# Four layers of graph network on 16 graphs: where the sort, the first graph's gates and the stores stand beside the attention

## The chip, the cores and the metric

The kernel runs on one core of one Trainium2 chip. The metric is the device time of one execution in microseconds (us). Before the change: 14,099.2 us, the median of three runs (14,098.43 to 14,108.07).

The engines, as the profile names them: PE is TensorE's matmuls and PEld its weight loads; DVE is VectorE; ACT is ScalarE; POOL is GpSimd; SP is SyncE, which here only issues DMA transfers. SPq, ACTq and POOLq are the queues from which the engines issue them.

## The reference

Sixteen graphs of 1024 nodes with 64 features each; `adj` is 16 x 1024 x 1024 float32. Each layer's result is added to its input and layer-normed.

```python
x = _layernorm(x + _L0_gnn_ref(x, adj, ...))            # normalised propagation, leaky ReLU
x = _layernorm(x + _L1_gnn_ref(x, adj, ...))            # attention
x = _layernorm(x + _L2_gnn_ref(x, adj, nodemask, ...))  # quantiles of the neighbours' features, MLP
x = _layernorm(x + _L3_gnn_ref(x, adj, ...))            # propagation
```

Layer 1 has 8 heads of 64. Its scores are gated by each node's own `gamma`, and the adjacency by the other half of it:

```python
gamma = jnp.exp(x @ W_gamma.T + b_gamma)
attn = g0 * attn + g1 * adj[:, None]
attn = jax.nn.softmax(attn, axis=-1)
out = jnp.einsum('bhnm,bhmd->bnhd', attn, v).reshape(b, n, H * DIM)
return out @ W_proj.T + b_proj
```

Layer 2 thins out each node's neighbours, sorts every feature over the remaining ones (`jnp.sort(vals, axis=2)`), and mixes the quantiles 0.25, 0.5 and 0.75 into an MLP with 128 hidden units.

## The kernel before

The graphs go through in eight pairs, and the outer loop over `p` runs stages of three pairs at once. Iteration `p` builds, in this order of the program: layer 0 of pair `p`, graph 0 and then graph 1 (`layer0`, with the thinning of the neighbours in `neighbours`); behind each of these graphs, layers 2 and 3 of one graph of pair `p - 2` (`ends`, `layers23`); the attention of pair `p`; the sort of pair `p - 1` (`middle`, `sort`); and pair `p - 1`'s quantile stage (`quantiles`). Iterations 0 and 1 have no `ends`, iteration 0 no sort and no quantiles, iteration 8 no layer 0 and no attention.

A planner puts this into order when the program is built: every instruction has its place in the program as its priority, and each engine gets a fixed list, drawn from the planner's own estimate of when inputs and buffers will be there. On the chip each engine works through its list and waits where an input isn't there. A manual dependency without a semaphore (`add_manual_dep` with `in_order`) holds one instruction behind another of the same engine in that list. Tiles come from pools with a number of buffers each; `bank` is a pool of four PSUM tiles that nearly every stage uses, `banks` one of two larger ones. Pools in SBUF share addresses over time: a tile waits for the tiles that lay where it lies.

**Attention.** For each graph of the pair, `keys_of` transposes x1, `gates` computes `gm` (L448 products, L452, the exponential L453) and the gated copy `xg` (L457), `queries_of` transposes that (both transposes are L277, their copies L278), and `gated` multiplies a block of the adjacency by its gate on GpSimd (L465). Then 64 steps follow: graph, head pair `hp` (4), half of the nodes `nh` (2), block `k4` (4). A step's parts on TensorE are put in sequence by hand (`then`): the scores of a step to come (L495, two heads), the transposes of this step's exponentials (L514), here and there a projection (L474) or values (L486), and at `k4 == 3` the scores of one step more and 32 products with the values (L522). Scores go through VectorE (L502: add the adjacency, row maximum) and ScalarE (L504: exponential), the transposes back through ScalarE (L516). `heads` (L537 to L547) multiplies by the output weights, sums over heads, and for `k == 3` adds bias and x1 and norms the layer into x2. At the end x2 is stored (L598), transposed (L603), copied (L604) and stored again as x2T (L605), both stores on SyncE's queue. The first graph's gates stand ahead of step 0, the second's at steps 10, 12 and 15.

**Sort.** A bitonic network over 1024 values in 55 steps, all on VectorE (L1034): three instructions a step (compare, minimum, maximum), each mask stored to DRAM, then the same 55 steps backwards on ranks with four instructions a step, each mask loaded again: 385 "swaps". `pace` holds every L502 of the attention, two per step:

```python
n = 4 * (next(steps_v) - EARLY) // 13
if 0 <= n < len(pace):
    tc.add_manual_dep(i.ins, pace[n].ins.name, in_order, reason="pace of the sort")
```

So the first `EARLY = 60` swaps are free and then 13 follow each two steps. Behind the sort the ranks are transposed (L1079, a `bank`), copied (L1081) and turned into words on VectorE (L1082 to L1102); `middle` is built behind the whole attention.

**Quantiles.** `load_matrix` loads the thinned adjacency `ndT` (8 loads on SyncE's queue); `elements` makes the one-hot words E from the words (L735 to L740, seven buffers); the first six half words are matmuls L808; then 96 steps of compare (L814), one-hot (L823), pick (L831) and matmuls L799, with the values' sums (L861, L880).

Of the kernel before, what the change touches and what calls it, by code (L numbers as in the profile page):

```python
# [25 lines left out]
P = 128  # L26
# [21 lines left out]
SECOND = (26, 28, 30, 38, 40, 45, 46, 47)  # L48
AHEAD = (10, 12, 15)
STEPS = 55  # L50
EARLY = 60
BN_EPS = 1e-5
# [57 lines left out]
def gnn_kernel(ctx: ExitStack, tc: tile.TileContext, a: dict, out: bass.AP):  # L110
# [147 lines left out]

    def layernorm(dst, y):

        st = small.tile([P, 4, 2, 6], F32, name="ln_st")
        mv = small.tile([P, 4, 2, 2], F32, name="ln_mv")
        rs = small.tile([P, 4, 2], F32, name="ln_rs")
        blocks = [(k, f) for k in range(4) for f in range(2)]
        for k, f in blocks:
            nc.vector.bn_stats(st[:, k, f, :], y[:, k, f, :])
            nc.vector.bn_aggr(mv[:, k, f, :], st[:, k, f, :])
        nc.scalar.activation(rs, mv[:, :, :, 1], AF.Sqrt, bias=eps)
        nc.vector.reciprocal(rs, rs)
        for k, f in blocks:  # L270
            nc.vector.tensor_scalar(dst[:, k, f, :], y[:, k, f, :], mv[:, k, f, 0:1], rs[:, k, f:f + 1],
                                    op0=ALU.subtract, op1=ALU.mult)
# [152 lines left out]
    def attention(nat, ip, adj, x1, x2):  # L425
# [4 lines left out]
        with (tc.tile_pool(name="att", bufs=2, reuse_waits="tile") as att,  # L430
              tc.tile_pool(name="att1", bufs=1, reuse_waits="tile") as att1):
            wqkv = twice(att1, "wqkv", a["WqkvT"], 3 * H * C)
# [3 lines left out]

            class Graph(SimpleNamespace):
                pass

            def keys_of(gr):  # L440
                gr.xT = att.tile([P, 512], F32, name="xT")
                transposed(gr.xT, gr.x1, then)

            def gates(gr):
                ps = [bank([P, 4, 2]) for f in range(2)]
                for k in range(4):
                    for f in range(2):
                        then(nc.tensor.matmul(ps[f][:, k, :], gr.xT[HALF[f], k * P:(k + 1) * P], wg[HALF[f]],  # L448
                                              start=True, stop=True))
                gr.gm = small.tile([P, 4, 2, 2], F32, name="gm")  # L450
                for f in range(2):
                    nc.vector.tensor_tensor(gr.gm[:, :, f], ps[f], bg_r[:, None, :].to_broadcast([P, 4, 2]), ALU.add)  # L452
                nc.scalar.activation(gr.gm, gr.gm, AF.Exp)  # L453
                gr.xg = att.tile(NODES, F32, name="xg")
                for k in range(4):
                    for f in range(2):
                        nc.vector.tensor_scalar(gr.xg[:, k, f, :], gr.x1[:, k, f, :], gr.gm[:, k, f, 0:1], C ** -0.5,  # L457
                                                op0=ALU.mult, op1=ALU.mult)

            def queries_of(gr):  # L460
                gr.xgT = att.tile([P, 512], F32, name="xgT")
                transposed(gr.xgT, gr.xg, then)

            def gated(gr, k):
                nc.gpsimd.tensor_scalar(gr.adj[k], gr.adj[k], gr.gm[:, k % 4, k // 4, 1:2], 1.0,  # L465
                                        op0=ALU.mult, op1=ALU.mult)
# [24 lines left out]
            def scores(gr, hp, k):  # L491
# [7 lines left out]
                for h in range(2):  # L499
                    s = att.tile([P, N], F32, name="s", bufs=4)  # L500
                    mx = att.tile([P, 1], F32, name="mx", bufs=4)
                    pace.append(nc.vector.tensor_tensor_reduce(  # L502
                        s, ss[h], gr.adj[k], -1.0, 3.0e38, ALU.add, ALU.min, mx))
                    nc.scalar.activation(s, s, AF.Exp, bias=mx, scale=-1.0,  # L504
                                         accum_out=gr.sm[:, k, 2 * hp + h:2 * hp + h + 1])
                    exps.append(s)
                return exps
# [19 lines left out]
            def heads(gr, k):  # L527
# [15 lines left out]
                nc.vector.tensor_reduce(gr.xg[:, k], t.rearrange("p f h q c -> p f c (h q)"), AX.X, ALU.add)  # L543
                if k == 3:
                    nc.vector.tensor_tensor(gr.xg, gr.xg, over_nodes(bp_r), ALU.add)
                    nc.vector.tensor_tensor(gr.xg, gr.xg, gr.x1, ALU.add)
                    layernorm(by_half(x2)[:, :, :, gr.bb, :], gr.xg)  # L547

            graphs = [Graph(bb=bb, x1=x1[bb], adj=list(adj), qk={}, sm=att.tile([P, NB, H], F32, name="sm"))
                      for bb in range(2)]  # L550
            g0, g1 = graphs
            keys_of(g0)
            gates(g0)
            queries_of(g0)
            for k in range(NB):
                gated(g0, k)
# [11 lines left out]
            for st, (gr, hp, nh, k4) in enumerate(steps):  # L568
# [7 lines left out]
                if at < 4:  # L576
                    if gr is g1:
                        heads(g0, at)
                    values(gr, at)
                if st in AHEAD:  # L580
                    (keys_of, gates, queries_of)[AHEAD.index(st)](g1)
# [16 lines left out]
            nc.sync.dma_start(x2_d[ds(ip * P, P)], x2)  # L598
# [6 lines left out]
            nc.sync.dma_start(x2T_d[ds(ip * P, P)], x2T)  # L605
        return pace
# [136 lines left out]
    def quantiles(ip, rk, u_w, b_w):  # L743
# [12 lines left out]
        with ExitStack() as es:  # L756
# [155 lines left out]
            load_matrix(graphs[0])  # L912
            more_words(2 * NW, nc.tensor.matmul)
# [61 lines left out]
    def layers23(agg1, agg2, tof, ip, bb):  # L975
# [16 lines left out]
        hT = agg1.tile([P, N], F32, name="hT")  # L992
# [6 lines left out]
        y = agg1.tile(NODES, F32, name="y2")  # L999
# [9 lines left out]
        sup = agg1.tile(NODES, F32, name="sup")  # L1009
# [14 lines left out]

    def sort(pool, key, pace, rk, u_w, b_w):
# [5 lines left out]
        steps_v = count()  # L1031

        def swap(*args):
            i = v.tensor_tensor(*args)  # L1034
            n = 4 * (next(steps_v) - EARLY) // 13
            if 0 <= n < len(pace):
                tc.add_manual_dep(i.ins, pace[n].ins.name, in_order, reason="pace of the sort")
# [39 lines left out]
        ps = bank([P, NB, P], F16)  # L1077
        for k in range(NB):
            nc.tensor.transpose(ps[:, k, :], rank[:, k * P:(k + 1) * P], identh)  # L1079
        r16 = pool.tile([P, 2 * G, NB, 4], U16, name="r16")  # L1080
        nc.scalar.copy(r16.rearrange("p g j c -> p j g c"), ps.rearrange("p j (g c) -> p j g c", c=4))  # L1081
        v.tensor_scalar(rk, r16, 5, None, op0=ALU.logical_shift_right)  # L1082
        v.tensor_scalar(r16, r16, 31, None, op0=ALU.bitwise_and)

        m = pool.tile([P, 2 * G, NB, 4], U16, name="m16")
        e = pool.tile([P, 2 * G, NB, 4], U16, name="e16")
        z = pool.tile([P, 2 * G, NB, 4], U16, name="z16")
        for w, first in ((2, 18), (1, 4), (0, 0)):
            dst = z if w == 0 else b_w[w - 1].bitcast(U16)
            if w < 2:  # L1090
                v.tensor_scalar(m, r16, float((4, 18)[w]), None, op0=ALU.is_lt)
            if w == 2:
                v.tensor_scalar(e, r16, 18.0, None, op0=ALU.is_ge)
            elif w == 1:
# [52 lines left out]
    for p in range(B // 2 + 1):  # L1147
        with double_banks(), ExitStack() as es:
# [20 lines left out]
            if p >= 1:  # L1169
                middle(srt, key, pace)  # L1170
# [35 lines left out]
```

## Time and profile before

| | us |
|---|---|
| median of three runs | 14,099.2 |
| the profiled execution | 14,101.11 |
| its span on the core | 14,099.3 |
| TensorE matmuls busy | 12,501.2 (89%) |
| VectorE busy | 10,732.0 (76%) |
| ScalarE busy | 7,312.0 (52%) |
| GpSimd busy | 598.3 (4%) |
| granted TensorE clock, mean | 0.937 |
| sort, L1034, all pairs | key 572.5, rank 391.6, mask 304.0, d 208.5 + 187.1 |
| attention's L502 / L504 | 1,211.9 / 1,179.4 |

A window line of the profile gives a stretch in us from the span's start, its length, then for each engine busy us and the number of instructions (waiting ones of the engine's sequencer included in a window of one line), the granted clock as a share of full speed, the mean share of the DMA engines, and GB/s. A timeline line gives start, duration, engine, line, operation, result and inputs, shapes, the number of merged instructions, and in brackets how long the engine was idle before and what ended that. A wait line gives who waited for whom, the total in us, how often and the longest.

The stages of one middle pair, from the lines' first and last times: layer 0 with layers 2 and 3 from 4102 to 4315, attention from 4315 to 4835, quantiles from 4845 to 5836. The pairs' first L808 products start at 1370.5, 3111.4, 4845.2, 6572.3, 8313.1, 10,053.8, 11,791.1 and 13,008.2; the sort of iteration 8, with no attention beside it, runs from 12,747 to 12,997.

### The profile page before, as it was taken

How to read it: one execution, taken by the hardware profiler on the slowest of the kernel's cores; microseconds unless marked ns; L12 is line 12 of the kernel's file. 1: busy time of each engine (PE TensorE's matmuls, PEld its weight loads, DVE VectorE, ACT ScalarE, POOL GpSimd, SP SyncE). 2: the span in 40 equal slices, each digit the busy share in tenths (PEclk: the TensorE clock that was granted, in tenths of full speed). 3: DMA queues.
4: the chain of work that ended last, by engine and by line, in shares of the span. 5: the costliest groups of instructions: out<-in, count | busy, mean ns of one | idle time of the engine just before them, and what ended most of it. 6: DMA issues, size and time to landing. Idle time of an engine off the chain costs nothing.

```text
span 14099.3 us, 207608 instructions
## 1 busy us (share of the span) xinstructions
PE 12501.2 (89%) x81450; PEld 5279.4 (37%) x81536; DVE 10732.0 (76%) x18475; ACT 7312.0 (52%) x13288; POOL 598.3 (4%) x932
## 2 busy tenths in 40 slices
PE   7978998889988899888998889978899798994998
PEld 3544333443334433344333443334433253331332
DVE  4476896768967688677885868858698586888885
ACT  4645554455545555355553555536555365552553
POOL 0001000000000000000000000000000000000000
PEclk8989999899998999989999899989999899997999
DMA  2021002200022000210002100021000310003001
GB/s 74 23 89 32 4 5 79 66 26 4 5 86 64 20 4 5 88 63 19 4 5 97 56 17 5 5 98 56 15 5 5 104 52 13 5 4 94 4 5 42
DMA packets 356344, 510.36 MB, mean 36 GB/s; under 512 B 124448, under 2 KB 279584, under 8 KB 353312
## 3 DMA queue, kind: packets, MB, share of 16 engines
q1 hardware_dynamic: 290960, 380.32, 8.3%
q10 hardware_dynamic: 34192, 87.14, 1.9%
q0 software_dynamic: 30208, 29.61, 0.9%
q8 instruction: 638, 10.45, 0.3%
q14 instruction: 346, 2.83, 0.1%
HBM read 380.32 MB, written 116.59 MB: 35 GB/s over the span
## 4 chain that ended last, share of the span: by engine, by line
PE 66%; DVE 21%; ACT 5%; DMA 4%; issue 3%; ACTq 0%; SPq 0%; DVEq 0%
PE bank L799 32%; PE acc L799 8%; PE bank L522 6%; PE banks L495 6%; PE bank L514 4%; PE wps L799 4%; DVE m L831 2%; DMA at<-in_adjT 2%; DVE key L1034 2%; DVE s L502 2%; ACT s L504 2%; PE bank L377 1%; DVE rem L356 1%; DVE rem L355 1%; PE bank L474 1%
## 5 line engine op out<-in xcount | busy, mean ns | idle before, releaser
L831 DVE TENSOR_TENSOR m<-V,oh 128x3072 bf16<-128x3072 bf16 x1536 | 2639.5, 1752 | 311.0 <-PE wps L799 286.6
L799 PE MATMUL bank<-ndT,E 128*128 128x512 fp8e4 x11904 | 2748.4, 380 | 6.6
L861 ACT ACTIVATE vals<-bank 128x512 f32<-128x512 f32 x3072 | 1592.9, 603 | 1403.0 <-PE bank L799 1401.1
L502 DVE CUSTOM_DVE_ANT_0 s<-banks,adj 128x1024 f32<-128x1024 f32 x1024 | 1211.9, 1220 | 956.2 <-PE banks L495 849.3
L809 ACT ACTIVATE V<-bank 128x512 uint16<-128x512 f32 x1536 | 911.7, 597 | 1805.6 <-PE bank L799 1651.4
L799 PEld LDWEIGHTS <-E 128*128 128x128 bf16 x11904 | 1116.7, 98 | 1786.6 <-issue 546.9
L823 ACT CAST oh<-bank 128x512 f16<-128x512 f32 x3072 | 1577.3, 602 | 290.1 <-PE bank L799 289.3
L504 ACT ACTIVATE s<-s,mx 128x1024 f32<-128x1024 f32 x1024 | 1179.4, 1153 | 744.6 <-DVE mx L502 744.5
L799 PE MATMUL bank<-oh,bd 128*128 128x512 f16 x6144 | 1484.7, 385 | 0.0
L495 PE MATMUL banks<-kT,qT 64*128 64x512 f32 x4096 | 1362.0, 656 | 131.6 <-DVE mx L502 126.6
L516 ACT COPY pT<-bank 128x512 f32<-128x512 f32 x2048 | 1071.2, 592 | 80.9 <-PE bank L514 73.1
L814 DVE TENSOR_TENSOR lt<-V,lim 128x2048 bf16<-128x2048 uint16 x768 | 934.5, 1217 | 222.1 <-PE bank L799 221.0
L514 PEld LDWEIGHTS bank<-ident,s 128*128 128x128 f32 x8192 | 922.2, 145 | 447.1 <-issue 250.5
L514 PE MATMUL bank<-ident,s 128*128 128x128 f32 x8192 | 1057.4, 284 | 15.9 <-ACT pT L516 15.2
L522 PE MATMUL bank<-pT,v 128*64 128x512 f32 x4096 | 966.0, 596 | 9.1 <-DVE t_pr L541 8.5
L799 PEld LDWEIGHTS <-bd 128*128 128x128 f16 x6144 | 543.6, 99 | 896.0 <-issue 363.4
L799 PE MATMUL bank<-lt,dif 128*128 128x512 bf16 x3072 | 816.4, 383 | 40.6 <-DVE lt L814 21.0
L799 PE MATMUL acc<-vals,bonesf 128*32 128x512 f32 x6144 | 849.8, 603 | 0.0
L495 PEld LDWEIGHTS banks<-kT,qT 64*128 64x128 f32 x4096 | 529.6, 200 | 660.8 <-issue 311.0
L799 PE MATMUL wps<-m,tonesb 128*32 128x512 bf16 x9216 | 646.2, 384 | 71.6 <-DVE m L831 71.6
L799 PE MATMUL bank<-r,pen 32*128 32x512 f16 x6144 | 490.6, 387 | 240.6 <-DVE r L718 226.5
L799 PE MATMUL acc<-oh,base 128*32 128x512 f16 x9216 | 641.6, 384 | 0.0
(242 smaller groups left out, 13175.6 us busy)
## 6 DMA issues: line engine op xcount, KB each, us to landing
at<-in_adjT SPq DMA_DIRECT2D x256, 512.0 KB, 5.2
masks_d<-mask SPq DMA_DIRECT2D x440, 128.0 KB, 1.7
mask<-masks_d SPq DMA_DIRECT2D x440, 128.0 KB, 2.1
adj<-in_adj SPq DMA_DIRECT2D x96, 512.0 KB, 6.0
ad<-in_adj ACTq DMA_DIRECT2D x64, 512.0 KB, 7.3
agg_d<-vals POOLq DMA_DIRECT2D x96, 256.0 KB, 2.3
agg<-agg_d ACTq DMA_DIRECT2D x16, 1536.0 KB, 7.1
nd_d<-nd SPq DMA_DIRECT2D x128, 128.0 KB, 1.9
```

Of the source, the lines that this page charges most:

```text
L495: then(nc.tensor.matmul(ss[h][:, hf * 512:(hf + 1) * 512], gr.qk[hp, 0][HALF[h], k * P:(k + 1) * P], gr.qk[hp, 1][HALF[h], hf * 512:(hf + ...
L502: pace.append(nc.vector.tensor_tensor_reduce(s, ss[h], gr.adj[k], -1.0, 3.0e38, ALU.add, ALU.min, mx))
L504: nc.scalar.activation(s, s, AF.Exp, bias=mx, scale=-1.0, accum_out=gr.sm[:, k, 2 * hp + h:2 * hp + h + 1])
L514: then(nc.tensor.transpose(ps[:, m, :], exps[h][:, (4 * mh + m) * P:(4 * mh + m + 1) * P], ident))
L516: nc.scalar.copy(pT[h][mh][:, :, k4 * P:(k4 + 1) * P], ps)
L522: then(nc.tensor.matmul(po[HALF[h]], gr.v[:, m, (2 * hp + h) * C:(2 * hp + h + 1) * C], pT[h][m // 4][:, m % 4, :], start=(m == 0), stop=( ...
L799: then(nc.tensor.matmul(*args, **kw))
L809: nc.scalar.activation(gr.V[g][:, w, cols], ps, AF.Copy, bias=OFF)
L814: nc.vector.tensor_tensor(u.lt, gr.V[g][:, None, 0, :].to_broadcast([P, 2, N]), gr.lim[q], ALU.is_lt)
L823: nc.scalar.copy(oh[:, kk, cols], ps)
L831: nc.vector.tensor_tensor(u.m[kk], gr.V[g].bitcast(BF), u.oh[s][:, kk, None, :].to_broadcast([P, NW, N]), ALU.mult)
L861: nc.scalar.activation(vals[t], ys[t], AF.Relu)
```

## The change

It has six parts. (1) The sort's pace counts steps instead of instructions of L502, and lets 3, 14, 3 and 3 swaps follow four steps in turn. (2) `middle` is built at step 58 of the attention instead of behind it. (3) The first graph's `keys_of`, `gates`, `queries_of` and `gated` are built right behind layer 0 of that graph; their tiles and `wqkv` lie in the pool `nat`, opened ahead of layer 0, and the second graph's in `att1`. (4) `heads` adds bias and x1 and takes the norm's statistics for each of four blocks instead of all at the end. (5) x2 and x2T are stored by GpSimd's queue. (6) At the start of a quantile stage the first six words E are built with high priority. For room, `hT`, `y2` and `sup` of layers 2 and 3 have one buffer instead of two.

```diff
+BESIDE = 58
+PACE = (3, 14, 3, 3)
...
-    def attention(nat, ip, adj, x1, x2):
+    def keys_of(gr, pool, then):
+        gr.xT = pool.tile([P, 512], F32, name="xT")
+        transposed(gr.xT, gr.x1, then)
...
+    def attention(nat, ip, graphs, wqkv, x2, beside):
...
-            wqkv = twice(att1, "wqkv", a["WqkvT"], 3 * H * C)
...
-                    pace.append(nc.vector.tensor_tensor_reduce(
-                        s, ss[h], gr.adj[k], -1.0, 3.0e38, ALU.add, ALU.min, mx))
+                    last = nc.vector.tensor_tensor_reduce(
+                        s, ss[h], gr.adj[k], -1.0, 3.0e38, ALU.add, ALU.min, mx)
...
+                pace.append(last)
                 return exps
...
-                nc.vector.tensor_reduce(gr.xg[:, k], t.rearrange("p f h q c -> p f c (h q)"), AX.X, ALU.add)
+                x = gr.xg[:, k]
+                nc.vector.tensor_reduce(x, t.rearrange("p f h q c -> p f c (h q)"), AX.X, ALU.add)
+                nc.vector.tensor_tensor(x, x, bp_r[:, None, :].to_broadcast([P, 2, C]), ALU.add)
+                nc.vector.tensor_tensor(x, x, gr.x1[:, k], ALU.add)
+                if k == 0:
+                    gr.norm = norm_tiles()
+                norm_stats(gr.norm, gr.xg, [k])
                 if k == 3:
-                    nc.vector.tensor_tensor(gr.xg, gr.xg, over_nodes(bp_r), ALU.add)
-                    nc.vector.tensor_tensor(gr.xg, gr.xg, gr.x1, ALU.add)
-                    layernorm(by_half(x2)[:, :, :, gr.bb, :], gr.xg)
...
+                    norm_apply(gr.norm, by_half(x2)[:, :, :, gr.bb, :], gr.xg)
...
             g0, g1 = graphs
-            keys_of(g0)
-            gates(g0)
-            queries_of(g0)
-            for k in range(NB):
-                gated(g0, k)
...
+                if st == BESIDE:
+                    beside(pace)
                 if st in AHEAD:
-                    (keys_of, gates, queries_of)[AHEAD.index(st)](g1)
+                    (keys_of, gates, queries_of)[AHEAD.index(st)](g1, att1, then)
...
-            nc.sync.dma_start(x2_d[ds(ip * P, P)], x2)
+            nc.gpsimd.dma_start(x2_d[ds(ip * P, P)], x2)
...
-            nc.sync.dma_start(x2T_d[ds(ip * P, P)], x2T)
-        return pace
+            nc.gpsimd.dma_start(x2T_d[ds(ip * P, P)], x2T)
...
             load_matrix(graphs[0])
+            with tc.high_priority():
+                while made < 2 * NW:
+                    elements()
             more_words(2 * NW, nc.tensor.matmul)
...
-        steps_v = count()
+        behind = chain([None] * EARLY, (p for p, n in zip(pace, cycle(PACE)) for _ in range(n)))

         def swap(*args):
             i = v.tensor_tensor(*args)
-            n = 4 * (next(steps_v) - EARLY) // 13
-            if 0 <= n < len(pace):
-                tc.add_manual_dep(i.ins, pace[n].ins.name, in_order, reason="pace of the sort")
+            p = next(behind, None)
+            if p is not None:
+                tc.add_manual_dep(i.ins, p.ins.name, in_order, reason="pace of the sort")
...
+                wqkv = twice(nat, "wqkv", a["WqkvT"], 3 * H * C)
                 with tc.tile_pool(name="l0", bufs=1, reuse_waits="tile") as l0:
                     tables = place_tables(l0)
-                    for bb in range(2):
-                        layer0(l0, tables, p, bb, None if bb else adj, x1[bb])
+                    for gr in graphs:
+                        gr.adj = list(adj)
+                        layer0(l0, tables, p, gr.bb, None if gr.bb else adj, gr.x1)
+                        if gr.bb == 0:
+                            for part in (keys_of, gates, queries_of):
+                                part(gr, nat, lambda i: None)
+                            for k in range(NB):
+                                gated(gr, k)
                         next(last, None)
...
             if p < B // 2:
-                pace = attention(nat, p, adj, x1, x2)
-            if p >= 1:
-                middle(srt, key, pace)
+                attention(nat, p, graphs, wqkv, x2, lambda pace: p and middle(srt, key, pace))
+            else:
+                middle(srt, key)
```

The functions `keys_of`, `gates`, `queries_of` and `gated` keep their instructions and only take the pool and the sequence as arguments; the last part of `sort`, from the transposes of the ranks on, becomes `words_of`, which `sort` calls at its end.

## The prediction

> **What bounds the kernel now.** I read the page first, then the waits, then windows over single stages, then timelines at the joints between stages. The page says TensorE is busy 89% of the span and ends most steps of the chain of work, so a gain has to be time in which TensorE waits, or runs at a lower granted clock. The 14,099.3 us hold eight attentions (graph pairs 0 to 7); pairs 1 to 7 each have a sort beside the attention and a quantile stage behind it. First products of the quantile stages (L808) start at 1370.5, 3111.4, 4845.2 ... : one pair is about 1735 us. I work on the pair whose attention runs from 4315 to 4823 and multiply.
>
> Waits of TensorE in that attention, up to the next stage (total us, times, longest):
>
> ```profile
> PE banks L495 <- DVE mx L502: 17.7, 11, 6.9
> PE bank L603 <- DVE x L271: 9.4, 1, 9.4
> ```
>
> The scores wait for VectorE, which alone serves both them (L502) and the sort. Windows over four steps each show it. Columns: window, length, then busy us with count for PE, PEld, DVE, ACT, POOL, then granted clock, DMA share, GB/s. The first two lines are pair 0, without a sort, the others the pair with one:
>
> ```profile
> 285.90:313.90 28.00, 26.12 (x137) 15.06 (x138) 9.51 (x16) 19.28 (x37) 0.00 (x0) 1.00 0.00 1
> 421.30:446.80 25.50, 25.37 (x134) 13.26 (x134) 10.00 (x17) 18.69 (x35) 2.23 (x2) 1.00 0.14 42
> ...
> 4398.80:4431.40 32.60, 29.55 (x137) 15.43 (x138) 32.22 (x54) 19.62 (x36) 0.00 (x0) 0.90 0.15 49
> 4552.10:4579.40 27.30, 27.10 (x134) 13.46 (x133) 20.61 (x43) 19.02 (x35) 2.64 (x3) 1.00 0.22 70
> 4740.10:4765.50 25.40, 25.37 (x134) 13.51 (x133) 9.51 (x16) 18.68 (x35) 0.00 (x0) 1.00 0.00 1
> ```
>
> Without a sort four steps take 25.4 to 28.6 us. Early in the sort VectorE is busy 32.2 of 32.6 us: it is the bound there and the clock falls to 0.90. From 4495 on the pace holds the sort back (26 swaps a window) and about 2 us remain. The sort is done at 4713, 13 steps before the end.
>
> **Part 1, gates beside layer 0.** The attention's start on TensorE:
>
> ```profile
> 4294.31 0.66 PE L284 MATMUL bank<-ident,x3T 128*128 128x128 f32 x4 [0.69 <-ACT x3T L1017]
> 4294.80 0.60 PE L277 MATMUL bank<-ident,x 128*128 128x128 f32 x4
> ...
> 4310.07 2.92 PE L474 MATMUL bank<-xgT,wqkv 64*128 64x512 f32 x3 [4.43 <-DMA wqkv<-in_WqkvT]
> ```
>
> The first graph's x1 was ready at 4165, yet its transposes (L277) come at 4294.8, right behind the last transposes of layers 2 and 3 (L284), though TensorE idles 5.15 us at 4268. L988 likewise follows layer 0's L284 at once (4134.72, then 4135.31), and hn's transposes of the second graph follow an L284 at 4205.6. I read this as: the four PSUM tiles "bank" are handed out in program order. After the change the projection (L474) is next behind that L284: 4294.9 instead of 4310.1, so **-15.2 us**; layer 0's last products end at 4264.2, so its memory is free. The wqkv wait (4.43 us) is in those 15.2.
>
> The same order costs something. The gates now stand between layer 0 of graph 0 and layers 2 and 3 of the older pair, so L988 gets its bank only when the gates' last transposes have theirs. In the old place that is 4294.80 to 4301.94 = 7.1 us; from x1's end, 4165.1, it gives 4172.2. L988 needs 6.4 us, the sum (L990) 0.7 us: L994 starts at about 4180 instead of
>
> ```profile
> 4174.86 1.13 PE L994 MATMUL banks<-oT,w 64*128 64x512 f32 x4
> ```
>
> so **+5.7**, and all of layer 0's second half is later by that. Together -9.5 us; bounds: +15 (the whole chain of 11.5 us, 4294.8 to 4306.3, and the exponential's table loads, 2 x 1.28, in the path) gives 0, and a fully hidden chain gives -15. Pairs 0 and 1 have no layers 2 and 3 there; the first scores come 14.5 us (203.7 to 218.2) and 18.7 us (838.8 to 857.5) behind layer 0's last products, in which the same chain lies; there I take -7.5 each.
>
> GpSimd's eight gatings (8.86 us) move along. Beside them VectorE's eight layer-norm scalings took
>
> ```profile
> 4305.25 5.12 DVE L271 TENSOR_SCALAR x<-y,ln_mv,ln_rs 128x64 f32<-128x64 f32 x8
> ```
>
> against 1.87 us for the same eight at 4273.12, so 3.25 us lost. That loss moves with them; I let it lie in the 5.7's range. The Trainium skill, "SBUF — State Buffer", section "Who interferes with whom", calls the port that VectorE and GpSimd share an exclusive lock whose loser fully blocks; by that the loss could be 8.9 us and the sum of this part -9.5 + 5.6 = -3.9. The row shows a slowing by 2.7, not a block.
>
> wqkv's two loads leave ScalarE's queue at 4305.7 (1.13 us of issue) and come ahead of layer 0, where the DMA share is 0.94 (4100 to 4150). If they land late there: 0.79 MB at that window's 320 GB/s, 2.5 us; queued behind them are ScalarE's sums of adj. The other way, they land while the last quantile steps run (0.28 from 4040 to 4100): 0. I take 0, bounds 0 to +8 with layer 0's tiles lying elsewhere than before.
>
> **Part 2, the sort's pace.** Swaps are 3 per step of the first half (1.93 us, 0.64 each) and 4 per step of the second (1.72 us, 0.43 each): 165 and 220. A step's two L502 take 2.29 us. New: 23 per four steps instead of 26, 14 of them behind the scores that precede the weighted products, where VectorE idles some 10 us (9.0 us of swaps fit), 3 behind each other one (1.9 + 2.3 = 4.2 us, under the 4.7 us that ScalarE needs a step, 18.7 a window / 4).
> - First windows: 60 swaps run unpaced and only 33 a window fit, so allowed swaps (60 + 5.75 a step) exceed done ones until about the fifth window. VectorE stays the bound: I take 0 for the four windows from 4367 to 4495 (excess over pair 0: 5.8, 4.6, 5.1, 4.8 us).
> - The opening, 52.5 us to the first weighted products against 42.2 in pair 0, holds the 6.9 us wait, since the sort starts with the scores. Now the scores start earlier while the sort's key still waits for layers 2 and 3's output: some 6 us of swaps leave. I take -5.
> - Seven windows from 4495 to 4713: excess 2.0, 1.4, 1.8, 0, 1.6, 3.6, 2.0 = 12.4; I take 70% back: -8.5.
> - The swaps go on to step 57: +1.5. The 13 instructions of words_of (6.85 us) and one ScalarE copy (1.0) now stand ahead of steps 59 on. VectorE is busy 9.5 of 24.6 us there, but a block of 6.85 in front of an L502 can hold TensorE: 0 to 6.9, I take +3.
> Sum -9 (bounds -38, all of the sort's slowing gone, to +8). Pair 1 is paced from its start and 24 us over pair 0: -15.
>
> **Part 3, the joint to the quantile stage.**
>
> ```profile
> 4832.50 2.15 PE L603 MATMUL bank<-ident,x 128*128 128x128 f32 x8 [9.38 <-DVE x L271]
> 4834.44 1.06 PE L1079 MATMUL bank<-identh,rank 128*128 128x128 f16 x8
> 4845.25 13.25 PE L808 MATMUL bank<-ndT,E 128*128 128x512 fp8e4 x48 [9.75 <-DVE E L736]
> ```
>
> The rank had been sorted since 4713, yet its transposes come behind x2's (bank order again); then ScalarE's copy, 13 VectorE instructions and the first E (4843.56 to 4845.2). After the change these words exist; the first six E (10 instructions, 5.5 us at 0.6 and 0.34 spacing) run in VectorE's 12.08 us idle at 4803. If that cover is gone: +5.5. L808 then follows L603: 4834.65 instead of 4845.25, **-10.6**. What is late next is the layer norm (the 9.38 wait), which stays: the two adds and the statistics move between the heads, but VectorE had no idle time between these, so 0 (+0.5). ndT must be there: its 8 loads were issued on SyncE at 4836.09, behind x2T's store; with both stores on GpSimd's queue nothing of the joint stands ahead. Were they still late (4.3 us of issue and 1.9 to land, as nd's stores): -3. From L808 to the first pick (28 us) TensorE is busy 24 of 25.4 us, so nothing more there.
>
> The stores themselves: 512 KB each, next read by SyncE some 480 us later or more; the loads of bd behind them on GpSimd's queue are used 12 quantile steps, 100 us, later. 0. The skill's same page, section "SBUF: two separate sides", speaks against them: a GpSimd-issued DMA can starve while VectorE holds the shared port. By that rule they land late, and the sum is the same.
>
> bufs=1 for hT, y2, sup: the next graph's L988 comes only behind the last L284, 0. Pair 8 (sort alone, 12747 to 12997) is unpaced as before: 0.
>
> **Sum.** Six pairs x (-9.5 - 9 - 10.6 = -29.1) = -175; pair 1: -7.5 - 15 - 10.6 = -33; pair 0: -7.5. Together -215 on the profiled execution's 14,101.1 us (span 14,099.3): 13,886; the median shown, 14,099.2, is 2 us lower, so I say 13,885. A change under 0.2% (28 us) could not be told from none.
>
> **Rivals.**
> - *More than that:* the early windows heal too (-15 a pair: 5.8 + 4.6 + 5.1 + 4.8 less a quarter), and L808 starts beside the heads' layer norm, behind 4823.1 (22 us early instead of 10.6). For: TensorE idles 9.38 us there. Against: L1079's place. 13,885 - 6 x 15 - 7 x 11.5 = 13,715; chance 0.22.
> - *Only the joint:* the pace gives nothing (VectorE's order is fixed by other things than the pace in the unpaced windows) and the gates' gain is eaten in layer 0: 14,101 - 74 = 14,027; chance 0.13.
> - *The sort becomes a stop:* the ranks' PSUM bank now stands in program order at step 58 of 64, so transposes of later steps wait until the last swap. Each swap still undone costs 0.43 us of TensorE. For: 23 instead of 26 a window, and a later key. Against: VectorE has 17 us a window for 10 us of swaps in the second half. It turns the sign from 68 undone swaps on (29.1 / 0.43); with 100 undone: 43 us x 7 - 215 = +86, 14,185; chance 0.08.
> - *Not done:* swaps could end where they did, if VectorE's order did not follow the pace; the trace shows 26 a window exactly, so it does; this case lies in the second rival.
> Forecast (13,760 to 13,990): 0.53. No measurable change, gains and losses even: 0.04.
>
> Range 13,650 to 14,030: it holds the forecast, most of the first two rivals, about 0.8. Faster 0.88 (0.53 + 0.22 + 0.13), same 0.04, slower 0.08.
>
> **What the profile after would show.** L474 directly behind L284 at each attention's start, L988 some 37 us later behind x1; windows from the sixth on at pair 0's 25.4 to 28.6; swaps until step 57; L808 directly behind L603 with no wait for E. Wrong if L808 starts ahead of L603 (bank order misread), if scores still wait for VectorE in the late windows, or if TensorE waits for the rank.

## The result and the profile after

The changed kernel takes 13,869.15 us (median of four runs, 13,839.85 to 13,885.19) against 14,103.17 us for the kernel before beside it: ratio 0.9832, 95% interval 0.9812 to 0.9851. The profiled execution took 13,882.45 us (span 13,880.5) against 14,101.11 (14,099.3): 218.8 us of span. 13,885 us was forecast.

The tables and rows below take pair 3 where they show one pair, as the prediction did; its attention starts at 4240.90 now. First TensorE's waits in that attention up to the next stage (total us, times, longest):

```profile
PE banks L507 <- DVE mx L514: 13.0, 10, 3.6
PE bank L618 <- DVE x L278: 8.4, 1, 8.4
```

The scores (L507, before L495) still wait for VectorE, but the longest wait is 3.6 instead of 6.9 us. The wait for the layer norm (L618) has stayed. Three windows of four steps at the same place as those of before (length, busy us of PE, PEld, DVE, ACT, POOL, clock, DMA share, GB/s):

```profile
4318.80:4351.50 32.70, 28.02 (x138) 16.38 (x138) 32.35 (x54) 19.87 (x36) 0.00 (x0) 0.95 0.15 49
4468.20:4494.50 26.30, 26.15 (x134) 13.16 (x134) 22.19 (x45) 18.79 (x36) 2.67 (x2) 1.00 0.22 71
4651.60:4677.00 25.40, 25.40 (x133) 13.52 (x133) 16.04 (x29) 18.69 (x35) 0.00 (x0) 1.00 0.00 1
```

The early window is as long as before (32.7): VectorE is still full. The middle one fell from 27.3 to 26.3, and swaps now reach the last one (VectorE 16.0 us busy, 9.5 before) without making it longer. The start of the attention on TensorE:

```profile
4235.40 1.11 PE L297 MATMUL bank<-ident,x3T 128*128 128x128 f32 x4 [0.68 <-ACT x3T L1034]
4236.44 2.08 PE L486 MATMUL bank<-xgT,wqkv 64*128 64x512 f32 x4
4238.31 1.92 PE L486 MATMUL bank<-xT,wqkv 64*128 64x512 f32 x4
4240.90 1.99 PE L507 MATMUL banks<-kT,qT 64*128 64x512 f32 x8 [0.67 <-ACT kT L489]
```

The projection (L486) stands directly behind L297, as forecast. The gates that stood between run in layer 0's first half:

```profile
4058.06 0.66 PE L297 MATMUL bank<-ident,hnT 128*128 128x128 f32 x4
...
4076.87 0.33 PE L290 MATMUL bank<-ident,x 128*128 128x128 f32 x1
...
4088.21 0.61 PE L449 MATMUL bank<-wg,xT 64*128 64x2 f32 x8
...
4095.88 0.61 PE L449 MATMUL bank<-wg,xT 64*128 64x2 f32 x8
...
4099.72 0.33 PE L290 MATMUL bank<-ident,xg 128*128 128x128 f32 x1 [1.76 <-DVE xg L458]
4099.98 1.80 PE L1005 MATMUL bank<-agg,tof 64*64 64x512 f32 x2
...
4110.65 1.13 PE L1011 MATMUL banks<-oT,w 64*128 64x512 f32 x4 [0.88 <-DVE oT L1007]
```

L1005 (before L988) starts only behind the first transpose of xg, and L1011 (before L994) comes 84.4 us behind the end of the older quantile stage (its last copy of values, L875, ends at 4026.3), not 72.5. Last the joint to the quantile stage:

```profile
4744.35 2.15 PE L618 MATMUL bank<-ident,x 128*128 128x128 f32 x8 [8.38 <-DVE x L278]
4747.35 12.87 PE L822 MATMUL bank<-ndT,E 128*128 128x512 fp8e4 x48 [0.86 <-DVE E L750]
```

The first product (L822, before L808) follows 3.0 us behind L618 instead of 12.75, with 0.86 us of wait for E.

Stage by stage, from the lines' first and last times (means of pairs 2 to 7, us):

| stage | before | after | moved | forecast |
|---|---|---|---|---|
| end of quantiles to first scores | 215.3 | 210.6 | -4.7 | -9.5 |
| first scores to first weighted products' end | 52.9 | 46.6 | -6.3 | -5 |
| to the last weighted products' end | 445.2 | 436.8 | -8.4 | -4 |
| to the first product of the quantile stage | 32.2 | 22.1 | -10.1 | -10.6 |
| quantile stage | 991.1 | 991.1 | 0.0 | 0 |

Six times -29.5 is -177; pairs 0 and 1 together gave -41 (forecast -40.6). Pair 0's scores came 3.3 us earlier (forecast 7.5), pair 1's 10.9 us, counted from pair 0's end (7.5), and its attention behind the opening got 18.0 shorter (15).

Counted from layer 0's last product, where the forecast had its 7.5, the scores came 11.6 and 15.7 us earlier (14.7 to 3.1 us and 19.0 to 3.3); layer 0 itself ended later by the rest. Its end in pair 0 is no fixed number: 206.2 to 215.5 us in the five kernels of the next section that do not differ up to there (after, even_pace, beside50, stores_sync, no_hi). The first stage of the table, too, has means of 208.2 to 210.6 us in these five, so differences of 2 us in it are not told apart.

### The profile page after: what moved, and what is told of

Same layout as the page of the kernel before. It is cut to its first block, busy times and chain, and to the rows that moved or that the text cites. A ratio compares the mean times of both kernels' runs of the same rounds, so it can differ in the third digit from the quotient of the medians.

```text
span 13880.5 us, 207747 instructions
## 1 busy us (share of the span) xinstructions
PE 12449.8 (90%) x81536; PEld 5250.0 (38%) x81536; DVE 10762.2 (78%) x18571; ACT 7311.2 (53%) x13292; POOL 623.3 (4%) x948
## 4 chain that ended last, share of the span: by engine, by line
PE 67%; DVE 19%; ACT 6%; DMA 3%; issue 3%; SPq 0%; ACTq 0%; DVEq 0%
PE bank L813 33%; PE acc L813 8%; PE bank L535 6%; PE banks L507 6%; PE bank L527 4%; PE wps L813 4%; ACT s L516 3%; DVE m L845 2%; DMA at<-in_adjT 2%; DVE key L1080 2%; PE bank L390 1%; DVE s L514 1%; ACT pT L529 1%; PE bank L486 1%; DVE rem L369 1%
## 5 line engine op out<-in xcount | busy, mean ns | idle before, releaser
L875 ACT ACTIVATE vals<-bank 128x512 f32<-128x512 f32 x3072 | 1593.5, 602 | 1401.5 <-PE bank L813 1396.9
L507 PE MATMUL banks<-kT,qT 64*128 64x512 f32 x4096 | 1315.4, 646 | 89.6 <-DVE mx L514 76.9
L527 PEld LDWEIGHTS bank<-ident,s 128*128 128x128 f32 x8192 | 907.5, 143 | 445.2 <-issue 234.4
L507 PEld LDWEIGHTS banks<-kT,qT 64*128 64x128 f32 x4096 | 521.1, 197 | 581.9 <-issue 310.5
```

Source lines behind the costliest of these rows:

```text
L507: then(nc.tensor.matmul(ss[h][:, hf * 512:(hf + 1) * 512], gr.qk[hp, 0][HALF[h], k * P:(k + 1) * P], gr.qk[hp, 1][HALF[h], hf * 512:(hf + ...
L527: then(nc.tensor.transpose(ps[:, m, :], exps[h][:, (4 * mh + m) * P:(4 * mh + m + 1) * P], ident))
L875: nc.scalar.activation(vals[t], ys[t], AF.Relu)
```

## The experiments

Twelve kernels ran, each beside the kernel before on the same chip, so ratios are to that. Measured:

| kernel | median us | ratio, 95% interval |
|---|---|---|
| after | 13,869 | 0.9832 (0.9812 to 0.9851) |
| pace_alone (before + pace) | 13,997 | 0.9934 (0.9922 to 0.9947) |
| joint_alone (before + joint) | 14,032 | 0.9960 (0.9946 to 0.9973) |
| wqkv_alone (before + early wqkv) | 14,046 | 0.9965 (0.9953 to 0.9978) |
| gates_back (after - gates' place) | 13,855 | 0.9833 (0.9819 to 0.9846) |
| wqkv_late (after - early wqkv) | 13,905 | 0.9866 (0.9853 to 0.9880) |
| gates_late (after, gates one place later) | 13,862 | 0.9838 (0.9825 to 0.9852) |
| gates_banks (gates_late, other PSUM tiles) | 13,813 | 0.9799 (0.9785 to 0.9812) |
| even_pace (after, no unpaced swaps) | 13,775 | 0.9771 (0.9758 to 0.9784) |
| both (gates_banks + even_pace) | 13,726 | 0.9738 (0.9724 to 0.9751) |
| beside50 (after, middle at step 50) | 13,976 | 0.9915 (0.9901 to 0.9929) |
| stores_sync (after, stores on SyncE) | 13,919 | 0.9876 (0.9862 to 0.9889) |
| no_hi (after, E without priority) | 13,864 | 0.9836 (0.9823 to 0.9850) |

My theory was the ledger on record: bank tiles in program order, and scores that wait for VectorE by the number of swaps. Its rivals were that one part does everything, or that a part does nothing.

**Pace alone.** The kernel before with the new `PACE` and `behind` in `swap`, on every second entry of `pace`.

> The kernel before with nothing but the new pace (23 swaps per four steps, 14 of them behind the scores that precede the weighted products). My terms: 0 in the first four windows, -8.5 us in the seven late windows of pairs 2 to 7, -15 us in pair 1, and no block of words_of ahead of the last steps; the opening keeps its time, as the gates still stand there: 6 x -8.5 - 15 = -66 us, about 14,035 us. If the opening's -6 us that the two traces show is the pace's too: 14,000. Rival, the scores wait for VectorE for another reason than the number of swaps behind each step: 14,100, no change, with the waits of L495 as before.

Measured 0.9934, about -93 us: more than the -66 of the late windows. The opening kept its 52.7 us, so that was not the pace's. From the first weighted products to the last the time fell by 13.4 us (445.2 to 431.8). The seven late windows gave 12.0 of them (217.0 to 205.0 us), all of their excess instead of the 70% that I took. Pair 1 gave 18.5 there.

**Joint alone.**

```diff
+                if st == BESIDE:
+                    beside(pace)
...
+            with tc.high_priority():
+                while made < 2 * NW:
+                    elements()
```

and the two stores on GpSimd's queue.

> The kernel before with nothing but the joint: middle beside step 58 of the attention, the first six E with high priority, the stores on GpSimd's queue; the old pace, the old gates, the layer norm in one piece. My term: -10.6 us at seven joints, L808 directly behind the last transposes of x2: -74 us, about 14,026 us; the words block ahead of the last steps may give back up to 3 us a pair (14,045). Rival, the joint gains only because the new pace lets the sort end later or because the norm is spread over the heads: under 5 us a joint, above 14,065 us.

Measured 0.9960, about -56 us. The joint took 22.4 us instead of 32.2 at all seven places (-9.8 each, -69); the attention ahead of it grew by 2.1 us, 1.1 of them in the window that holds the words (24.6 to 25.7, the same in the changed kernel). Theory right.

**Gates put back.**

```diff
-                        if gr.bb == 0:
-                            for part in (keys_of, gates, queries_of):
-                                part(gr, nat, lambda i: None)
-                            for k in range(NB):
-                                gated(gr, k)
...
+            for part in (keys_of, gates, queries_of):
+                part(g0, nat, then)
+            for k in range(NB):
+                gated(g0, k)
             project(g0, 0, 0)
```

> The kernel after with the first graph's gates put back ahead of step 0 of the attention (their tiles and wqkv stay in the early pool). My term on record, -9.5 us in six pairs and -7.5 us in two, comes back: +72 us, 13,941 us. The ledger of the two traces has a smaller one, -4.7 us in layer 0's stage (six pairs), -3.3 and -10.5 us in pairs 0 and 1: +42 us, 13,911 us; with the opening's -6 us, if that belongs to the gates, +78 us, 13,947 us. Rival, the gates' place is worth nothing: 13,869 us.

Measured 0.9833 against 0.9832: my theory fell, and its rival held. With wqkv early, the gates' new place is worth nothing that can be measured (the two intervals leave room for some 30 us). Yet this kernel keeps the shorter start (210.1 us) and the shorter opening (45.7), which pace and joint alone do not have. Its rows show what is left:

```profile
4202.45 0.66 PE L297 MATMUL bank<-ident,x3T 128*128 128x128 f32 x4 [0.69 <-ACT x3T L1038]
4202.94 0.60 PE L290 MATMUL bank<-ident,x 128*128 128x128 f32 x4
...
4214.46 2.08 PE L486 MATMUL bank<-xgT,wqkv 64*128 64x512 f32 x4 [0.67 <-ACT xgT L291]
...
4218.91 2.08 PE L507 MATMUL banks<-kT,qT 64*128 64x512 f32 x4 [0.67 <-ACT kT L489]
```

The gates' chain is back, and L486 waits 0.67 us for xgT where before it waited 4.43 us for wqkv. So the new theory: of Part 1 only wqkv's early load counts. VectorE's order differs as well. Its list is fixed when the program is built, so it is the planner's estimate that changed and not a race on the chip. In the kernel before:

```profile
4314.80 0.69 DVE L1034 TENSOR_TENSOR mask<-key 128x512 f16<-128x512 f32 x1 [4.43 <-DMA key<-x2T_d]
...
4324.33 1.22 DVE L502 CUSTOM_DVE_ANT_0 s<-banks,adj 128x1024 f32<-128x1024 f32 x1
```

and with the gates put back:

```profile
4222.83 1.23 DVE L514 CUSTOM_DVE_ANT_0 s<-banks,adj 128x1024 f32<-128x1024 f32 x1 [4.33 <-PE banks L507]
...
4225.13 0.69 DVE L1084 TENSOR_TENSOR mask<-key 128x512 f16<-128x512 f32 x1
```

Fifteen swaps ran ahead of the first reduction (4314.80 to 4324.33), in each of the pairs 2 to 7; now the first scores are served ahead of the sort.

**wqkv alone, and wqkv late.** The first adds to the kernel before only this; the second takes it out of the changed kernel:

```diff
+                wqkv = twice(nat, "wqkv", a["WqkvT"], 3 * H * C)
                 with tc.tile_pool(name="l0", bufs=1, reuse_waits="tile") as l0:
```

> The kernel before with nothing but wqkv's two loads ahead of layer 0 (its tile in the pool nat). Theory, formed on the run with the gates put back: the gates' place is worth nothing, wqkv's place is. Two terms in pairs 2 to 7: the 4.4 us in which L474 waits for wqkv go, and with the scores that much ahead of the sort's key, whose load lands 3 to 4 us behind them, the opening falls from 52.9 to about 46 us, as the first scores are served before the first swaps. Together -11 us in six pairs, nothing in pairs 0 and 1, where xgT is what L474 waits for: -66 us. Rival, the opening's -7 us needs the new place of middle or the shorter norm: -4.4 x 6 = -26 us. Second rival, wqkv ahead of layer 0 delays layer 0's loads by as much as it gains: 0.

> The kernel after with wqkv's loads back behind layer 0, at the head of the attention; the gates stay beside layer 0. Theory: the projection, now ready some 5 us behind the last L297, waits for wqkv, whose tile comes free only with layer 0's last products and which needs 3.5 to 6 us to land (issued at 4305.7, landed at 4311.7 in the kernel before, 41 us behind layer 0's last products since ScalarE's queue holds it in program order): +4 to +12 us in six pairs and the opening's -6 us lost, +60 to +110 us over the kernel after. Rival, wqkv's place is worth nothing and the gates' place is what gains: +0 to +10 us.

Alone: 0.9965, about -49 us; start 215.3 to 210.9 (-4.4), opening 52.9 to 46.7 (-6.2), as the theory has them; the attention behind the opening took 2.1 us back. Late: 0.9866; the start is back at 215.3 us (+4.7), but the opening stayed at 46.2, against my expectation. There the gates stand beside layer 0, and the sort still started 5.3 us behind the scores. So the theory was too narrow: either move, wqkv's or the gates', brings the opening's gain. What goes with it in every kernel is VectorE's order: with fifteen swaps ahead of the first reduction the opening takes 52.7 to 53.0 us (before, pace_alone, joint_alone), with none 44.7 to 47.2 (all the others). Early wqkv is worth 10 us a pair at the start and in the opening when the gates stand late, and 5 when they stand early.

The parts alone give -93 - 56 - 49 = -198 us. gates_back holds these three, the norm spread over the heads, the gates' tiles in `nat` and the single buffers, and has -235. Of the rest, some 26 us lie in pairs 0 and 1: there the scores follow layer 0's last product after 2.8 us in both, where early wqkv alone has 13.4 and 18.3 (14.7 and 19.0 before). The tiles of the gates lie outside layer 0's memory, and their transposes run among layer 0's last products. That was read from the traces and not tried by itself.

**Gates one place later, and with other PSUM tiles.** In gates_late `next(last, None)` moves ahead of the gates' block; in gates_banks also:

```diff
-        ps = bank([P, 512])
+        ps = banks([P, 2, 512])[:, 0] if wide else bank([P, 512])
```

and one `banks` tile for the two gate products.

> The kernel after with the first graph's gates written behind the older pair's first graph (layers 2 and 3) instead of ahead of it. Theory: the 12 us by which L1011 of the first older graph comes later than in the kernel before are the gates' chain standing ahead of L1005 in TensorE's order; behind it the chain hides in the waits of layers 2 and 3, and the start of the attention moves by -7 to -12 us in six pairs: 13,797 to 13,827 us. Rival, those 12 us come from something else (VectorE's products of rem, layer norm beside GpSimd, wqkv's loads): 13,869 us, and the gates only stand in the way of hn's transposes of the second graph, up to +10 us a pair, 13,930 us.

> The kernel with the gates behind the older pair's first graph, but with their PSUM tiles taken from the two double banks (banks) instead of the four single ones (bank). Theory: with the single banks the gates' chain stands in the path wherever it is written, since bank tiles come in program order (hn's transposes of the second graph wait for xg's, 10 us); the double banks are unused while layers 2 and 3 propagate, so the chain finishes there and hn's transposes follow L297 directly: the start of the attention comes about 10 us earlier in six pairs, -60 us against the kernel after; the same in pairs 0 and 1 or a few us. Rival, the order is not the banks' but that of TensorE's own queue or of VectorE: no change, within 15 us of the kernel after.

gates_late: 0.9838, no gain. L1011 is back at 71.7 to 75.9 us, but now the second half is late by about as much (start 208.3 us, inside the spread given above), and the rows show the queue:

```profile
4120.84 1.12 PE L297 MATMUL bank<-ident,x3T 128*128 128x128 f32 x4 [0.68 <-ACT x3T L1034]
4121.75 1.06 PE L290 MATMUL bank<-ident,x 128*128 128x128 f32 x4
...
4130.16 0.45 PE L290 MATMUL bank<-ident,xg 128*128 128x128 f32 x1 [4.80 <-DVE xg L458]
...
4132.28 0.47 PE L290 MATMUL bank<-ident,xg 128*128 128x128 f32 x1 [0.63 <-DVE xg L458]
4132.55 0.42 PE L290 MATMUL bank<-ident,hn 128*128 128x128 f32 x1
```

x1 had been ready for some 40 us, yet its transposes come behind L297, and hn's come behind xg's. In gates_banks the same work is done beside the propagation (L390):

```profile
4111.17 1.11 PE L290 MATMUL banks<-ident,x 128*128 128x128 f32 x4
4112.21 4.81 PE L390 MATMUL bank<-at,sup 128*64 128x512 f32 x12
4116.95 1.06 PE L453 MATMUL banks<-wg,xT 64*128 64x2 f32 x16
...
4125.79 0.48 PE L290 MATMUL banks<-ident,xg 128*128 128x128 f32 x1
...
4131.53 0.66 PE L297 MATMUL bank<-ident,x3T 128*128 128x128 f32 x4 [0.69 <-ACT x3T L1038]
4132.02 0.60 PE L290 MATMUL bank<-ident,hn 128*128 128x128 f32 x4
```

0.9799: the start falls from 210.6 to 200.5 us, 10.1 in six pairs, as the theory said. Against the kernel before that is 14.8 us (215.3 to 200.5), nearly all of the 15.2 that the prediction gave for the chain at its old place: the same operations, in other PSUM tiles, cost next to nothing. It was the bank tiles, then, and not a queue of TensorE or VectorE, that put the chain in the path. That it is their order and not their number rests on the rows of gates_late, where x1's transposes came only behind L297; a larger pool was not tried.

**Even pace.**

```diff
-EARLY = 60
-PACE = (3, 14, 3, 3)
+EARLY = 0
+PACE = ((3, 13, 3, 3), (4, 18, 5, 5))
```

with the second tuple from step 30 on.

> The kernel after with no swap unpaced (EARLY 0) and the pace by VectorE's time instead of by count: 22 swaps per four steps while a swap takes 0.64 us, 32 per four steps once it takes 0.43 us; the last swap is allowed at step 58. Theory: the first four windows of a pair (32.2, 32.7, 30.7, 30.5 us against 25.5 to 28 without a sort) are slow only because 60 unpaced swaps pile up; with 14.2 us of swaps and 9.5 us of reductions in a window of 25.4 us they fall by 3 to 4 us each, the middle ones rise by up to 1 us: -8 to -14 us in pairs 2 to 7, -50 to -80 us against the kernel after; pair 1, whose 60 swaps ran in layer 0, may lose up to 10 us. Rival, the sort becomes a stop: the ranks' bank and the words stand at step 58, and every swap still undone then costs 0.43 us of TensorE, 10 to 40 us a pair: +70 to +280 us.

Measured 0.9771, more than my theory's upper end. The four windows behind the opening together, first of the changed kernel, then of this one (columns as above):

```profile
4286.60:4412.70 126.10, 113.08 (x553) 62.78 (x554) 123.73 (x219) 78.08 (x143) 0.00 (x0) 0.95 0.17 57
```

```profile
4258.60:4367.30 108.70, 105.38 (x555) 61.73 (x554) 93.30 (x162) 76.45 (x143) 0.00 (x0) 0.98 0.11 36
```

162 VectorE instructions instead of 219 in the same sixteen steps, and 108.7 instead of 126.1 us; pair 0, without a sort, takes 107.0. Pair 1 of the changed kernel shows which half of the edit does this: it has the uneven pace too, but its first 60 swaps ran beside layer 0, and it takes 109.7 us. So these windows were slow by the backlog. TensorE's busy time fell too, from 113.1 to 105.4 us, at a granted clock of 0.98 instead of 0.95. By the means the four windows gave 18.9 us (126.2 to 107.3) and the whole stretch behind the opening 15.0 (436.8 to 421.8): 3.9 come back, most where swaps of 0.64 us meet the faster pace: the window 4422 to 4451 took 29.2 us where pair 0 has 25.4. Pair 1 lost 6 us in its attention but starts 7 us earlier, counted from pair 0's end: its first 60 swaps ran in layer 0 before.

**Both gains together.** gates_banks with the even pace, its change at step 32.

> The kernel after with both edits that gained on it: the gates behind the older pair's first graph with their PSUM tiles from the double banks, and the even pace, with the change from 22 to 32 swaps per four steps at step 32 instead of 30 (at 30 the slow swaps were not all done and a window took 29.5 us instead of 25.4). If the two gains add: the gates' tiles gave -10.1 us in six pairs (-56 us), the even pace -15 us in the same six and some -6 in pair 1 (-94 us), and step 32 returns up to 3 us a pair: 13,869 - 56 - 94 - 0 to 18 = 13,700 to 13,720 us. Rival, they cover the same time (the later key helps only while the start is late): 13,760 to 13,780 us, as the even pace alone.

They add: 0.9738, 13,726 us. Against the changed kernel that is 0.9738 / 0.9832 = 0.990, worked out from the two ratios; the two gains alone, 0.33% and 0.61%, sum to the 0.94% measured. The later change of pace did not help (the slow window's mean went from 29.5 to 29.9 us, another's from 28.1 to 30.2).

**Middle at step 50.** `BESIDE = 50`.

> The kernel after with middle written beside step 50 instead of 58. This asks for the price of the rival on record, the sort as a stop. With only 51 steps to be paced by, the last 30 or so swaps stand unpaced, 22 of them in one block, and the ranks' PSUM bank lies in program order between steps 50 and 51. Theory (banks in program order): TensorE's transposes of the next steps wait until the block (22 x 0.43 = 9.5 us), the ranks' transposes and their copy (2 us) are done, less some 3 us of reserve: +6 to +12 us in seven pairs, +40 to +85 us over the kernel after. Rival (the ranks' bank is handed out only when it is asked for): 0 to +10 us.

Measured 0.9915, some +117 us over the changed kernel: the sort as a stop, and dearer than I expected.

```profile
PE bank L1046 <- DVE rank L1080: 14.8, 1, 14.8
```

TensorE waits 14.8 us once in each of seven pairs. Between VectorE's last reduction ahead of it and the transposes run 29 swaps, 4649.2 to 4664.2: 15.0 us, 0.52 each, more than the 0.43 that I had taken. I had counted one block of 22 and subtracted a reserve that is not there.

**Stores on SyncE.** Both `nc.gpsimd.dma_start` of x2 and x2T back to `nc.sync`.

> The kernel after with the stores of x2 and x2T back on SyncE's queue. On record: the loads of ndT stood behind x2T's store on SyncE, 8 issues of 0.5 us and 1.9 us to land; with the stores there again the first product of the quantile stage waits for ndT instead of following the transposes of x2: up to +3 us at seven joints, +20 us. Rival, the loads' order on SyncE is the planner's and does not change, or E is the later one: 0 us.

Measured 0.9876, +0.44% over the changed kernel, where I had +20 us at most.

```profile
4757.05 2.15 PE L618 MATMUL bank<-ident,x 128*128 128x128 f32 x8 [8.46 <-DVE x L278]
4763.98 0.59 PE L822 MATMUL bank<-ndT,E 128*128 128x512 fp8e4 x1 [4.79 <-DMA ndT<-nd_d]
```

The joint grows by 3.8 us, and by 2.4 more up to the first pick, since the products also wait for later slices of ndT: 6.2 x 7 = 43 us. The 0.44% are 62 us; the rest lies within the intervals. The loads of ndT issue at 4760.3 here, behind the stores, which wait for the layer norm; in the changed kernel they issue at 4683.4, 64 us ahead of the first product.

**E without priority.** The `with tc.high_priority()` block taken out.

> The kernel after without the high priority of the first six E. On record: the six E take 5.5 us of VectorE and fit into its idle 12 us ahead of the joint; without that cover +5.5 us at the joint, but only the first E (0.6 us) stands ahead of the first product, so the first product loses 1 to 2 us and the rest runs beside the products: +7 to +38 us at seven joints. Rival, without priority they stand behind the heads' layer norm in VectorE's order and are needed there anyway: 0 us.

Measured 0.9836, joint 22.1 us as with it: the priority does nothing once the words stand at step 58. The rival was right.

## Why the prediction was right

The sum was right (-215 forecast, -219 in the span, -234 in the medians), and so were the mechanisms of the opening, the pace and the joint. That it came so close is in part luck: in six pairs the start gave 29 us less than forecast (4.8 each), and the opening and the attention 34 us more (1.3 and 4.4 each).

- **Part 1, gates beside layer 0: -9.5 forecast, -4.7 measured, and from another cause.** The gain at the attention's start came as forecast: from the second half's L297 to the scores 21.3 us before, 4.4 after (means), 16.9 less. The step that failed is the price of the order, +5.7. I took the chain at its old length of 7.1 us from x1's end to xg's first transpose. In layer 0 that took 13.7 us (4086.1 to 4099.7), 7.7 of them between the gates' first and second products (4088.21 and 4095.88), among which layer 0's own products run; xg's last transposes come 4 us later still, and most of L1005 behind them. L1011 came 11.0 us later (73.1 to 84.1) and the second half's L297 12.1. That eats all but 4.7 us, and these are about wqkv's wait (4.4), which I had inside the 15.2 and which gates_back keeps without moving the gates.
- **wqkv's loads: 0 taken, and 0 is what they cost ahead of layer 0** (the first half's L1011 stands at 71 to 75 us in gates_back, as before).
- **The opening: -5 forecast, -6.3 measured.** The reason on record, scores ahead of the sort's key, is what the rows show; the early wqkv gives it (wqkv_alone, 46.7 us), and so do the early gates (wqkv_late, 46.2).
- **Early windows: 0 forecast**, 128.4 to 126.2 us measured. The excess of allowed swaps was the right reason; even_pace shows that the same windows need 107 us when nothing is unpaced. The rival "more than that" had the mechanism of such a gain, but this change does not release it.
- **Late windows: -8.5 forecast, -12.0 in the pace alone.** The term was mis-sized: all of the excess went. The sign named on record, scores that still wait for VectorE there, is all but gone (0.5 us once, 1.6 in four waits before). In the changed kernel 4 us of it are missing again, in two windows (45.9 to 48.7, 27.2 to 28.7) whose length differs as much between kernels in pair 0 without a sort (45.9 to 48.7). What sets it stays open; the norm's statistics between the heads, which lie in the first of them, were not tried by themselves.
- **Words ahead of the last steps: +3 forecast, +1.1** (24.6 to 25.7). Swaps up to step 57: +1.5 forecast, +1.0 (27.2 to 28.2).
- **Joint: -10.6 forecast, -10.1**; 0.86 us of wait for E was left where I had none. The cover that I priced at 5.5 us for the first E was no condition (no_hi).
- **Stores: priced as at most -3 a joint if ndT were late.** The mechanism was named, its size was 6.2. The rule cited there, that a store from GpSimd's queue can starve (the Trainium skill, "SBUF — State Buffer", section "SBUF: two separate sides"), shows little here: the eight stores of x2 landed 3.0 to 4.3 us after issue, those of x2T 3.1 to 7.4, on SyncE in stores_sync 2.6 to 2.7 and 2.9 to 5.2, and nobody waits for them.
- **The gatings beside VectorE: a wrong reading.** The row of 5.12 us was read as a slowing by 2.7 and not a block. Instruction by instruction it is a block, one gating at a time:

```profile
L271 DVE TENSOR_SCALAR x<-y,ln_mv,ln_rs x8: 300/627/1182, 4305.3 to 4310.1; 128x64 f32<-128x64 f32 x8
...
L465 POOL TENSOR_SCALAR adj<-adj,gm x8: 1112/1118/1171, 4300.6 to 4308.3; 128x1024 f32<-128x1024 f32 x8
```

  Each line gives the shortest, median and longest duration in ns. Four scalings took 0.95 to 1.18 us, about a whole gating each, and each ended with one; the other four, behind the last gating, took 0.30, as alone (0.31). The size taken, 3.25 us, was right.
- **The sort becomes a stop** did not happen at step 58; at step 50 it does, at 14.8 us for 29 swaps, 0.51 us each instead of the 0.43 on record.

## What to carry to other kernels

A pool of PSUM tiles handed out in program order is a queue: work written ahead of a critical chain in the same pool stands in front of it even when its data has long been there, and moving it only moves the toll; taking its tiles from a pool that is idle at that time removed it. A pace should start with the first instruction: an even pace without sixty unpaced swaps gained 15 us in each of six pairs. Whether it should also count time rather than instructions was not tried apart. Ask of a load that is late whether its tile can lie in a pool that is opened earlier, and of a store that waits for the last result what is queued behind it.

## What the hardware showed unexpectedly

In a stretch bound by VectorE, TensorE's own work was slower too: the same 16 steps of products were 117.0 us busy at clock 0.89 before, 113.1 at 0.95 after, 105.4 at 0.98 with the even pace, and 103.6 at 1.00 in pair 0 of the kernel before, without a sort. The first of these:

```profile
4367.50:4494.70 127.20, 116.99 (x554) 63.88 (x553) 123.56 (x227) 77.60 (x143) 0.00 (x0) 0.89 0.17 57
```

So TensorE lost more there than the time in which it stood idle; that its waits are what lowered the clock was not tried by itself. And a loss that I had let move with GpSimd's gatings did not: the eight scalings of the layer norm at the attention's start took 5.12 us beside them before and 1.87 us now. In layer 0 the gatings (8.87 us for eight, 8.86 before) lie beside xg's eight products, as they did before (4.61 us both times), and then beside an idle VectorE, which waits 6.8 us for L1005.
